# Half of an input projection made during the first scan, through device memory

## The chip, the core and the metric

The kernel runs on one core of a Trainium2 chip. The time is device microseconds of one execution, from three runs of the kernel before: 3769.12 us in the median (3767.9 to 3770.96). The profile comes from one further execution with the hardware profiler on.

The core has five engines, each with its own in-order queue of instructions: TensorE (PE in the profile; its weight loads are PEld), VectorE (DVE), ScalarE (ACT), GpSimd (POOL) and SyncE (SP, which here only issues DMAs). Sixteen DMA engines carry what is issued from SP and ACT.

## The reference

The input x holds 32 sequences of 256 tokens of 256 channels. First comes a selective state-space block, then two layers of local attention with a gated feed-forward, and the input is added at the end:

```python
xr, gate = jnp.split(x @ W_in.T, 2, axis=-1)          # 512 channels each
xr = xr + t_emb[:, None, :]
xc = silu(causal_depthwise_conv(xr, 4 taps) + b_conv)
xn = layernorm(xc)
Bm, Cm, dt = jnp.split(xn @ W_xproj.T, 3, axis=-1)    # 16 states each
...
h = jnp.clip(h * ad[:, :, None] + bd[:, :, None] * xt[:, None, :], -10.0, 10.0)
yt = jnp.einsum('bd,bdh->bh', ct, h)                  # 256 steps in order
...
return (y + D * xn) * silu(gate) @ W_out.T
# then, twice: attention over windows of 128 tokens, feed-forward with gelu
```

The scan over time is sequential: 256 steps for each sequence. All arithmetic that matters here is 32-bit.

## The kernel before

**Tiling.** The 32 sequences go in four groups of eight (`GB`). A scan step works on [128, 512]: 16 states times 8 sequences on the partitions, 512 channels along the free dimension. A group's 256 steps are cut into eight chunks (`NCH`) of 32 steps (`CH`). For each chunk, some 40 steps ahead of its first, the kernel loads x (`load_x`), projects it (`project`, four times for the convolution's half and four times for the gate's half), convolves, normalises, writes the normalised rows to device memory (`norm_out`, tensor `xnd`), and works out the factors of each step.

**A step.** `step` (line 660) is one custom VectorE instruction: it adds a scaled row to the state and clips it. The row of step t is the normalised token of eight sequences, repeated for 16 states. Normally `load_rows` (line 629) fetches it from `xnd` with a DMA of 256 KB that repeats it, and `scale_row` (line 650) scales it on ScalarE. During the first group's scan (`alone`), `by_tensor` picks steps with `t % NQ < XR`, that is two of every four, for another way: `spread_rows` (line 637) repeats the row with TensorE, two 32-row matmuls for two steps, out of a compact copy `xq` (`load_skip`), and ScalarE scales it out of PSUM. Row tiles (`xrep`) rotate through six buffers. `read_out` (line 672) turns the states of four steps into outputs, four matmuls of 32 columns each.

**Stages.** The scan of group 1 runs with nothing beside it. After it, attention and feed-forward of group g run beside the scan of group g+1. The last group's attention and feed-forward run alone.

**Order.** Each piece of the scan is put at a slot (`at(slot, function, ...)`), where slot s of a group stands beside step s; group g is shifted by 256 g slots (`scan_slots`). The second agenda of a group, lines 832 to 855, holds what a step needs of TensorE and of the row loads. `scan_to` advances the slots along the stages of attention and feed-forward. From this written order a planner fixes the order in each engine's queue and draws all waits; it may bring an instruction forward that has its inputs and its buffer (loads of the weights, put at slots from 100 on, stand at 10 to 32 us of the trace). It holds instructions back to each other's order where `keep_in_program_order` says so. A buffer of a tag with `bufs=n` is handed on when its last reader is done.

**Buffers that the change touches.** Tag `xg` (two buffers: the x of a chunk, which is read by the convolution's projections at slots s0 - 40 to s0 - 34 and by the gate's at s0 + 13 to s0 + 18), tag `rot` (four: `xq` in the first scan, rotary products later), tag `pT` (six: the weights of `spread_rows` in the first scan, attention's probabilities later), and the eight PSUM banks (`bank`).

Of the kernel before, what the change touches and what calls it, by code (L numbers as in the profile page):

```python
# [10 lines left out]
FP = mybir.dt.float32  # L11
# [8 lines left out]
P = 128  # L20
S = 256
DM = 256
KM = DM // P
DI = 512
NC_ = DI // P
NS = 16
GB = 8
CH = 32
NCH = S // CH
TB = P // GB  # L30
NQ = 4
# [3 lines left out]
XR = 2  # L35
TAPS = 4
# [16 lines left out]
def bc(ap, axis, n):  # L53

    ap = ap.unsqueeze(axis)
    shape = list(ap.shape)
    shape[axis] = n
    return ap.broadcast_to(shape)
# [15 lines left out]
def kernel(  # L74
# [29 lines left out]
    nc = tc.nc  # L104
    B = xT.shape[2]
    L = wqkv.shape[1]
    NG = B // GB

    const = ctx.enter_context(tc.tile_pool(name="const", bufs=1))
    def loaded(src, shape, name, q=None):  # L110
        t = const.tile(shape, FP, tag=name, name=name)
        (q or nc.scalar).dma_start(out=t, in_=src)
        return t
# [22 lines left out]
    w_in_sb = loaded(w_inT, [P, KM, 2 * DI], "w_in_sb", nc.sync)  # L136
# [26 lines left out]
    for j in range(NJ):  # L163
# [18 lines left out]
        out=mask_t[:, 0:W], in_=mask_t[:, 0:W], compare_op=ALU.is_ge, fill=MASKED_LOW,  # L182
# [3 lines left out]
        out=mask_t[:, W : 2 * W], in_=mask_t[:, W : 2 * W], compare_op=ALU.is_ge,  # L186
# [27 lines left out]
    for i in range(2):  # L214
        t = const.tile([P, NI * (P + GB)], FP, tag=f"ly{i}", name=f"ly{i}")
# [3 lines left out]
    def program(ctx, exact):  # L219
        rpool = ctx.enter_context(tc.tile_pool(name="res", bufs=1, reuse_waits="tile"))  # L220
        wpool = ctx.enter_context(tc.tile_pool(name="weights", bufs=1, reuse_waits="tile"))
        sp = ctx.enter_context(tc.tile_pool(name="sp", bufs=1, reuse_waits="tile"))
        sm = ctx.enter_context(tc.tile_pool(name="sm", bufs=2, reuse_waits="tile"))
        hp = ctx.enter_context(tc.tile_pool(name="hp", bufs=8, reuse_waits="tile"))
        xp = ctx.enter_context(tc.tile_pool(name="xp", bufs=6, reuse_waits="tile"))
        dp = ctx.enter_context(tc.tile_pool(name="dp", bufs=3, space=DRAM))
        ap_ = ctx.enter_context(tc.tile_pool(name="at", bufs=2, reuse_waits="tile"))
        aw = ctx.enter_context(tc.tile_pool(name="aw", bufs=3, reuse_waits="tile"))
        ps_w = ctx.enter_context(tc.tile_pool(name="psw", bufs=8, space=PSUM, reuse_waits="tile"))

        def bank(pool, tag, name):
            return pool.tile([P, DI], FP, tag=tag, name=name)
# [140 lines left out]
        def group_scan(g):  # L373
# [8 lines left out]
            alone = g == 0  # L382

            agendas = [{}]
            state = {"p": one}
            ck = [{} for _ in range(NCH)]

            def at(s, what, *args):
                agendas[-1].setdefault(s, []).append(partial(what, *args))
# [12 lines left out]
                ck[c]["ps", ch] = ps  # L402


            def load_x(c):
                xg = sp.tile([P, KM, GB, CH], FP, tag="xg", name="xg", bufs=2)
                for k in range(KM):
                    nc.sync.dma_start(
                        out=xg[:, k], in_=xT[:, k, b0 : b0 + GB, c * CH : (c + 1) * CH]
                    )  # L410
                ck[c]["xg"] = xg
                ck[c]["carry"] = sm.tile(
                    [P, NC_, GB, TAPS - 1], FP, tag="carry", name="carry"
                )

            def conv_in(c, ch):
                if ch == 0:
                    ck[c]["xc"] = sp.tile([P, NC_, GB * CH], FP, tag="xc", name="xc")
                ps = ck[c].pop(("ps", ch))
                xr = sp.tile([P, GB, TAPS - 1 + CH], FP, tag="xr", name="xr", bufs=2)  # L420
                if c == 0:
                    nc.gpsimd.memset(xr[:, :, 0 : TAPS - 1], 0.0)
                else:
                    nc.gpsimd.tensor_copy(xr[:, :, 0 : TAPS - 1], ck[c - 1]["carry"][:, ch])
                nc.vector.tensor_add(
                    xr[:, :, TAPS - 1 :],
                    ps.rearrange("p (b t) -> p b t", b=GB),
                    bc(cond_sb[:, ch, b0 : b0 + GB], 2, CH),
                )
                acc = sp.tile([P, GB, CH], FP, tag="acc", name="acc", bufs=2)  # L430
                nc.gpsimd.tensor_scalar(  # L431
                    acc, xr[:, :, 0:CH], wc_sb[:, ch, 0:1], bconv_sb[:, ch : ch + 1],
                    ALU.mult, ALU.add,
                )
                if c < NCH - 1:
                    nc.gpsimd.tensor_copy(ck[c]["carry"][:, ch], xr[:, :, CH:])
                ck[c]["xr", ch] = xr, acc
# [183 lines left out]
                return ck[c]["xnd"].rearrange("(b t) d -> b t d", b=GB)  # L621

            def by_tensor(t):
                return alone and t % NQ < XR

            def load_rows(c, t):
                xr = xp.tile([P, DI], FP, tag="xrep", name="xrep")
# [18 lines left out]
            def scale_row(c, t):  # L646
                if by_tensor(t):
                    ck[c]["rep", t] = xp.tile([P, DI], FP, tag="xrep", name="xrep")
                bx = ck[c]["rep", t]
                scaled = nc.scalar.activation(  # L650
                    bx, ck[c].pop(("bx", t), bx), AF.Copy, scale=ck[c]["beta"][:, t : t + 1]
                )
                if not alone:

                    tc.keep_in_program_order(scaled)
# [140 lines left out]
            for c in range(NCH):  # L796
                s0 = c * CH
                for hb in range(CH // TB):
                    s = s0 + hb * TB
# [5 lines left out]
                for ch in range(NC_):  # L805
                    at(s0 - 38 + 2 * ch, conv_in, c, ch)
                    at(s0 - 37 + 2 * ch, conv_taps, c, ch)
                    at(s0 - 36 + 2 * ch, conv_th, c, ch)
                    at(s0 - 35 + 2 * ch, conv_out, c, ch)
# [5 lines left out]
                for j in range(NJ):  # L815
                    s = s0 - 26 + 4 * j
# [15 lines left out]
            agendas.append({})  # L832
            for c in range(NCH):
                s0 = c * CH
                at(s0 - 43, load_x, c)
                for ch in range(NC_):
                    at(s0 - 40 + 2 * ch, project, c, ch)
                for ch, s in enumerate((13, 16, 17, 18)):
                    at(s0 + s, project, c, NC_ + ch)
                at(s0 - 27, raw_sums, c)  # L840
                for j in range(NJ):
                    at(s0 - 26 + 4 * j, norm_turn, c, j)
                at(s0 - 8, figures_out, c)
                for t in range(CH):
                    if not by_tensor(t):
                        at(s0 + t - 6, load_rows, c, t)
                    if by_tensor(t) and t % XR == 0:
                        at(s0 + t - 4, spread_rows, c, t)
                    at(s0 + t - 2, scale_row, c, t)
                for hb in range(CH // TB):  # L850
                    s = s0 + hb * TB
                    at(s - 9 if alone else s + 7, load_skip, c, hb)
                    at(s + 23, out_turn, c)
                for d in range(KM):
                    at(s0 + 43 + 2 * d, project_y, c, d)

            return agendas

        def scan_slots(groups):


            slots, scans = {}, [group_scan(g) for g in groups]
            for part in range(2):
                for i, agendas in enumerate(scans):
                    for s, what in agendas[part].items():
                        slots.setdefault(i * S + s, []).extend(what)
            for s in range(min(slots), max(slots) + 1):
                for what in slots.get(s, ()):
                    what()
                yield s  # L870


        ys, res, wt = {}, {}, {}

        def load_res(g, b):
            t = rpool.tile([P, KM, 1 + S], FP, tag=f"res{b}", name=f"res{b}")
# [90 lines left out]
        if exact:  # L967
# [4 lines left out]
                out=mask[:, 0:W], in_=mask[:, 0:W], compare_op=ALU.is_ge, fill=MASKED,  # L972
# [3 lines left out]
                out=mask[:, W : 2 * W], in_=mask[:, W : 2 * W], compare_op=ALU.is_ge, fill=MASKED,  # L976
# [425 lines left out]
        s0 = done[0]  # L1402
        group, reload = ST * L * GB, ST * (L * GB - GB + 6) + 2
        for t in range(max(stages) + 1):
# [3 lines left out]
            g, r = divmod(t + 1 + group - reload, group)  # L1408
# [10 lines left out]
    with tc.If(fits > 0) as which:  # L1419
        with ExitStack() as es:  # L1420
            program(es, False)
    with which.Else():
        with ExitStack() as es:
            program(es, True)
# [108 lines left out]
```

## Time and profile before

| | |
|---|---|
| median of three runs | 3769.12 us (3767.9 to 3770.96) |
| profiled execution, its own time | 3770.68 us |
| its span, first to last instruction | 3768.9 us |
| TensorE busy in the span | 3644.0 us (97%), granted clock 0.986 |
| VectorE busy | 2639.5 us (70%) |
| ScalarE busy | 2163.9 us (57%) |
| GpSimd busy | 1796.0 us (48%) |
| DMA, mean over the span | 103 GB/s, 387.53 MB |
| row loads (`xrep<-xnd`) | 896 of 256 KB |
| step 1 of the first scan starts at | 54.3 us |

A row of the profile names line, engine and operation, then output and inputs by tile name, the shape and the count; after the bar come busy time, the mean in ns, and the time that the engine was idle just before such instructions, with what ended the idle time. Busy time of TensorE counts the modelled end of each matmul, and where matmuls overlap, their common time once. A 32-bit matmul leaves two records.

### The profile page before, as it was taken

The page shows a single profiled execution, that of the slowest core. Times are in us where ns is not written, and L with a number is a line of the kernel's source. Part 1 is how long each engine was busy: PE and PEld are TensorE (multiplying, and loading weights), DVE is VectorE, ACT ScalarE, POOL GpSimd, SP SyncE. Part 2 cuts the span into 40 slices and gives each one's busy share as a digit, 9 for nine tenths or more (in the row PEclk, how much of TensorE's full clock was granted, in tenths as well). Part 3 has the DMA queues.
Part 4 walks back from the last instruction along what each step waited for, and adds up shares of the span by engine and source line. Part 5 has one row for each costly group of instructions (what it writes and reads, how often), then busy time and mean ns, then how long its engine had stood idle before and what let it go on. Part 6 is the DMA issues. An engine that isn't in the chain of part 4 may idle for free.

```text
span 3768.9 us, 57035 instructions
## 1 busy us (share of the span) xinstructions
PE 3644.0 (97%) x20028; PEld 2255.5 (60%) x20028; DVE 2639.5 (70%) x5177; ACT 2163.9 (57%) x3769; POOL 1796.0 (48%) x1776
## 2 busy tenths in 40 slices
PE   7999989999999999999999999999999999999998
PEld 3333345666666666666666666666666666666666
DVE  6988888788778777777777777777776444444443
ACT  3555556666666666656666665666566444444442
POOL 4443365544455455545445555545454444433441
PEclk8999999999999999999999999999999999999999
DMA  5444555344454545444444545444353111011101
GB/s 149 114 119 117 135 155 135 101 119 116 116 130 123 145 120 150 106 108 114 112 120 110 147 119 138 115 101 116 108 130 109 54 43 50 12 29 38 29 26 35
DMA packets 396250, 387.53 MB, mean 103 GB/s; under 512 B 176355, under 2 KB 256052, under 8 KB 395828
## 3 DMA queue, kind: packets, MB, share of 16 engines
q1 hardware_dynamic: 311506, 371.80, 37.1%
q10 hardware_dynamic: 84450, 12.01, 2.0%
q8 instruction: 161, 2.64, 0.3%
q14 instruction: 133, 1.09, 0.1%
HBM read 348.05 MB, written 34.08 MB: 101 GB/s over the span
## 4 chain that ended last, share of the span: by engine, by line
PE 68%; DVE 16%; POOL 6%; ACT 4%; issue 3%; DMA 3%; SPq 0%; ACTq 0%; POOLq 0%; DVEq 0%
PE ps_qkv L907 14%; PE pa L1246 13%; PE po_f L1274 8%; PE y L672 5%; DVE h L660 5%; PE ps_wo L957 4%; PE sc L1113 4%; PE ov L1151 3%; DVE acc L442 3%; PE ps_out L750 3%; PE ps_in L395 3%; PE tr_qk L946 2%; POOL rn L939 2%; PE rs L1132 2%; PE sc L1106 2%
## 5 line engine op out<-in xcount | busy, mean ns | idle before, releaser
L660 DVE CUSTOM_DVE_ANT_0 h<-h,xrep,lim 128x512 f32<-128x512 f32 x1024 | 936.5, 915 | 238.7 <-ACT xrep L650 207.7
L907 PE MATMUL ps_qkv<-qkv,res 128*128 128x512 f32 x1536 | 712.1, 600 | 23.6 <-DVE ag L1262 18.2
L650 ACT ACTIVATE xrep<-xrep,beta 128x512 f32<-128x512 f32 x896 | 622.5, 717 | 113.2 <-DMA xrep<-xnd 71.0
L1246 PE MATMUL pa<-hT,w 128*128 128x256 f32 (+1 forms) x3072 | 684.4, 385 | 0.3 <-DVE zT L741 0.2
L1246 PEld LDWEIGHTS pa<-hT,w 128*128 128x128 f32 (+1 forms) x3072 | 498.4, 178 | 159.6 <-issue 44.1
L931 POOL TENSOR_TENSOR rot<-rot,swp 128x512 f32<-128x512 f32 x256 | 335.2, 1309 | 368.9 <-DVE swp L928 223.7
L939 POOL TENSOR_TENSOR rn<-ss,neg_half 128x8 f32<-128x8 f32 x256 | 460.3, 1798 | 17.8 <-DVE ss L937 7.9
L907 PEld LDWEIGHTS ps_qkv<-qkv,res 128*128 128x128 f32 x1536 | 278.0, 191 | 300.5 <-issue 260.5
L1274 PE MATMUL po_f<-ag,w 128*128 128x256 f32 (+1 forms) x1536 | 386.8, 393 | 13.5 <-DVE ag L1262 8.9
L1203 POOL TENSOR_TENSOR rstd<-ve,neg_half 128x1 f32<-128x1 f32 x128 | 81.2, 634 | 645.7 <-DVE ve L1201 642.8
L672 PE MATMUL y<-h,ly 128*32 128x512 f32 x2048 | 372.7, 620 | 10.6 <-DVE h L660 9.8
L1274 PEld LDWEIGHTS po_f<-ag,w 128*128 128x128 f32 (+1 forms) x1536 | 273.0, 189 | 120.0 <-issue 54.6
L1262 DVE SCALAR_TENSOR_TENSOR ag<-pa,b_sb,ag 128x256 f32<-128x256 f32 (+1 forms) x448 | 212.5, 474 | 171.6 <-ACT ag L1254 168.0
L940 POOL TENSOR_TENSOR rot<-rot,rn 128x512 f32<-128x512 f32 x256 | 301.1, 1176 | 20.0
L1254 ACT ACTIVATE ag<-pa,b_sb 128x256 f32<-128x256 f32 x320 | 150.7, 471 | 268.1 <-PE pa L1246 266.0
L395 PE MATMUL ps_in<-xg,w_in_sb 128*128 128x256 f32 x1024 | 282.8, 407 | 19.1 <-DMA xg<-in_xT_dram 14.9
L920 ACT ACTIVATE sq<-ps_qkv 128x512 f32<-128x512 f32 x256 | 151.7, 596 | 236.5 <-PE ps_qkv L907 200.1
L395 PEld LDWEIGHTS ps_in<-xg,w_in_sb 128*128 128x128 f32 x1024 | 189.9, 198 | 142.4 <-issue 41.2
L442 DVE SCALAR_TENSOR_TENSOR acc<-xr,wc_sb,acc 128x256 f32<-128x256 f32 x384 | 189.5, 496 | 91.7 <-POOL acc L431 89.6
L923 DVE TENSOR_TENSOR rot<-ps_qkv,rc_sb 128x512 f32<-128x512 f32 x256 | 175.3, 685 | 82.9 <-ACT sq L920 82.9
L957 PE MATMUL ps_wo<-oT,wo 128*128 128x256 f32 x1024 | 231.6, 379 | 0.0
L450 ACT ACTIVATE th<-acc 128x256 f32<-128x256 f32 x128 | 53.0, 414 | 308.3 <-DVE acc L442 255.0
(146 smaller groups left out, 5672.4 us busy)
## 6 DMA issues: line engine op xcount, KB each, us to landing
xrep<-xnd SPq DMA_DIRECT2D x896, 256.0 KB
rb<-inv SPq DMA_DIRECT2D x128, 256.0 KB
xnd<-xn SPq DMA_DIRECT2D x64, 256.0 KB
qkv<-in_wqkv_dram SPq DMA_DIRECT2D x24, 512.0 KB
xd<-xnd SPq DMA_DIRECT2D x192, 64.0 KB
w<-in_w_dram SPq DMA_DIRECT2D x80, 128.0 KB
xg<-in_xT_dram SPq DMA_DIRECT2D x64, 128.0 KB
ys<-yo ACTq DMA_DIRECT2D x64, 128.0 KB
```

The costliest lines, as they stand in the source:

```text
L395: nc.tensor.matmul(ps, w_in_sb[:, k, ch * P : (ch + 1) * P], ck[c]["xg"][:, k], start=(k == 0), stop=(k == KM - 1),)
L442: nc.vector.scalar_tensor_tensor(acc, xr[:, :, k : k + CH], wc_sb[:, ch, k : k + 1], acc, ALU.mult, ALU.add,)
L650: scaled = nc.scalar.activation(bx, ck[c].pop(("bx", t), bx), AF.Copy, scale=ck[c]["beta"][:, t : t + 1])
L660: nc.vector._custom_dve(TENSOR_ADD_SAT, out=h_new, in0=state["h"], in1=bx, s0=ck[c]["lim"][:, 0, t : t + 1], s1=ck[c]["lim"][:, 1, t : t + 1],
L672: nc.tensor.matmul(ck[c]["y", hb][32 * q : 32 * q + 32, :], ly[hb % 2][:, 32 * t : 32 * t + 32], ck[c].pop(("h", hb * TB + t)), start=(i = ...
L907: nc.tensor.matmul(ps, res[b][:, k, t0 : t0 + W], wt["qkv", a][:, k], start=(k == 0), stop=(k == KM - 1),)
L931: nc.gpsimd.tensor_add(rot, rot, swp)
L939: nc.gpsimd.tensor_tensor(rn, ss, neg_half, ALU.pow)
L940: nc.gpsimd.tensor_mul(rot, rot, bc(rn, 2, DH))
L957: nc.tensor.matmul(po[:, d], wt["wo", 0][:, c, d * P : (d + 1) * P], oT[:, c, :], start=(c == 0), stop=(c == NC_ - 1),)
L1246: nc.tensor.matmul(pg if x else pa, wt["w1", m][:, k, x], self.h[:, k], start=(k == 0), stop=(k == KM - 1),)
L1274: nc.tensor.matmul(self.po[:, d], wt["w2", 0][r0 : r0 + n, m, d * P : (d + 1) * P], self.ag[m][r0 : r0 + n], start=(m == 0), stop=(m == le ...
```

## The change

Three things are done.

1. For groups 2 to 4 (the code's g = 1 to 3) the convolution's half of the input projection is no longer made ahead of each chunk. 48 units of work are put evenly over the first scan's slots -30 to 220: `ahead_load` fetches the x of a chunk (for every second unit, two DMAs of 128 KB), `ahead_project` makes two of the four channel blocks of a chunk into one PSUM bank, `ahead_copy` copies the bank to SBUF on ScalarE, and `ahead_put` stores it to device memory, 256 KB a unit. Later, at slots s0 - 44 and s0 - 42 of the chunk, `load_projected` fetches both units of the chunk into buffers of tag `xg`, and `conv_in` reads its addend there and not from PSUM.
2. `load_x` of these groups moves from slot s0 - 43 to s0 + 6, since only the gate's half still needs x; the small tile `carry` is made in `conv_in`.
3. `by_tensor` takes `t % (2 * NQ) < XR`: in the first scan two of every eight rows are spread by TensorE, and six of eight are loaded.

```diff
+            def ahead_load(u):
+                if u % 2 == 0:
+                    gg, c = 1 + u // 2 // NCH, u // 2 % NCH
+                    t = ap_.tile([P, KM, GB, CH], FP, tag="rot", name="xa", bufs=4)
+                    for k in range(KM):
+                        nc.sync.dma_start(
+                            out=t[:, k],
+                            in_=xT[:, k, gg * GB : (gg + 1) * GB, c * CH : (c + 1) * CH],
+                        )
+                    state["xa", u // 2] = t
+            def ahead_project(u):
+                ps = bank(ps_w, "w", "ps_a").rearrange("p (r n) -> p r n", r=2)
+                for r in range(2):
+                    ch = 2 * (u % 2) + r
+                    for k in range(KM):
+                        nc.tensor.matmul(
+                            ps[:, r],
+                            w_in_sb[:, k, ch * P : (ch + 1) * P],
+                            state["xa", u // 2][:, k],
+                            start=(k == 0),
+                            stop=(k == KM - 1),
+                        )
+                state["pa", u] = ps
+            def ahead_copy(u):
+                t = aw.tile([P, 2, GB * CH], FP, tag="pT", name="xs_a", bufs=6)
+                nc.scalar.copy(t, state.pop(("pa", u)))
+                state["ta", u] = t
+            def ahead_put(u):
+                d = dp.tile([P, 2, GB * CH], FP, tag=f"ahead{u}", name=f"ahead{u}", bufs=1)
+                nc.sync.dma_start(out=d, in_=state.pop(("ta", u)))
+                projected[u] = d
+            def load_projected(c, i):
+                t = sp.tile([P, 2, GB * CH], FP, tag="xg", name="xp", bufs=2)
+                nc.sync.dma_start(out=t, in_=projected[((g - 1) * NCH + c) * 2 + i])
+                for r in range(2):
+                    ck[c]["ps", 2 * i + r] = t[:, r]
...
             def by_tensor(t):
-                return alone and t % NQ < XR
+                return alone and t % (2 * NQ) < XR
...
-                at(s0 - 43, load_x, c)
-                for ch in range(NC_):
-                    at(s0 - 40 + 2 * ch, project, c, ch)
+                at(s0 - 43 if alone else s0 + 6, load_x, c)
+                if alone:
+                    for ch in range(NC_):
+                        at(s0 - 40 + 2 * ch, project, c, ch)
+                else:
+                    for i in range(2):
+                        at(s0 - 44 + 2 * i, load_projected, c, i)
...
+            if alone:
+                n = (NG - 1) * NCH * 2
+                for u in range(n):
+                    s = -30 + u * (NCH * CH) // n
+                    at(s - 5, ahead_load, u)
+                    at(s, ahead_project, u)
+                    at(s + 2, ahead_copy, u)
+                    at(s + 4, ahead_put, u)
```

More of the change, by code (lines that the diff above doesn't have):

```diff
@@ L411, in load_x @@
                 ck[c]["xg"] = xg
-                ck[c]["carry"] = sm.tile(
-                    [P, NC_, GB, TAPS - 1], FP, tag="carry", name="carry"
-                )
             def conv_in(c, ch):
                 if ch == 0:
+                    ck[c]["carry"] = sm.tile(
+                        [P, NC_, GB, TAPS - 1], FP, tag="carry", name="carry"
+                    )
                     ck[c]["xc"] = sp.tile([P, NC_, GB * CH], FP, tag="xc", name="xc")
@@ L870, in scan_slots @@
                 yield s
-        ys, res, wt = {}, {}, {}
+        ys, res, wt, projected = {}, {}, {}, {}
         def load_res(g, b):
```

## The prediction

> **What bounds the kernel now.** I read three things in this order: the table of engine times by stage, to see where TensorE has room; the sequence of TensorE instructions in two of the stages, for the price of what moves; and the groups and waits of the first scan, for what sets its pace. The stages are: set-up (0 to 54 us), the first scan with nothing beside it (54 to 440), the hand-over (to 620), the scans of groups 2 to 4 beside attention and feed-forward (to 2930), and the last group's attention. Each row gives length, busy us of each engine, clock, DMA share and GB/s.
>
> ```profile
> core 0: us, PE busy (x) PEld busy (x) DVE busy (x) ACT busy (x) POOL busy (x), PEclk, DMA share, GB/s
> 0.00:54.00 54.00, 29.18 (x116) 22.02 (x116) 24.24 (x71) 8.04 (x17) 21.49 (x64) 0.75 0.67 174
> 54.00:440.00 386.00, 355.46 (x1315) 134.14 (x1315) 345.30 (x623) 227.99 (x425) 157.77 (x194) 0.94 0.45 118
> 440.00:620.00 180.00, 159.11 (x726) 77.08 (x726) 154.24 (x290) 99.02 (x182) 106.07 (x110) 0.92 0.55 145
> 620.00:2930.00 2310.00, 2271.88 (x13151) 1462.10 (x13150) 1752.70 (x3413) 1447.79 (x2525) 1177.05 (x1131) 1.00 0.46 120
> ```
>
> In the long stage TensorE is busy 98% and VectorE 76%: TensorE's work is the time. In the first scan TensorE is at 92% and VectorE at 89%: neither is free. The change moves TensorE work from the first kind of stage into the second, so everything turns on how much of it the first scan swallows.
>
> Prices, from the TensorE sequence of the main stage and of the first scan (start, length with its tail, instruction, records; every f32 matmul is two records):
>
> ```profile
> 2027.85 1.99 PE L395 MATMUL ps_in<-xg,w_in_sb 128*128 128x256 f32 x8
> 2029.68 0.38 PE L1223 MATMUL tp_hn<-ident,hn 128*128 128x128 f32 x2
> ...
> 301.98 1.13 PE L637 MATMUL bx<-xq,rep_w 32*128 32x512 f32 x4
> 303.04 1.05 PE L672 MATMUL y<-h,ly 128*32 128x512 f32 x4
> 304.02 1.12 PE L637 MATMUL bx<-xq,rep_w 32*128 32x512 f32 x2
> 305.07 1.05 PE L672 MATMUL y<-h,ly 128*32 128x512 f32 x2
> ```
>
> Eight projection records take 1.83 us from start to next start. Two spread rows (x4) take 1.06 us, but one (x2) takes 1.05 as well. The same holds for read-out (y): two matmuls cost no more than one when they stand together.
>
> Groups of the first scan (count, busy us, mean ns, idle before):
>
> ```profile
> L660 DVE CUSTOM_DVE_ANT_0 h<-h,xrep,lim 128x512 f32<-128x512 f32 x250 | 231.7, 927 | 8.2 <-DVE h L660 1.9 <-PE ps_in L395 0.6 <-PE y L672 0.3
> L672 PE MATMUL y<-h,ly 128*32 128x512 f32 x488 | 144.4, 648 | 4.8 <-DVE h L660 4.0
> L650 ACT ACTIVATE xrep<-xrep,beta 128x512 f32<-128x512 f32 x127 | 88.9, 715 | 73.6 <-DMA xrep<-xnd 60.1 <-DVE beta L598 4.4 <-DVE h L660 3.9
> L637 PE MATMUL bx<-xq,rep_w 32*128 32x512 f32 x252 | 80.8, 639 | 0.0
> ```
>
> and what the queue of SyncE (which issues every row load) waits for there (us, times, longest):
>
> ```profile
> SPq L629 <- DVE h L660: 147.8, 77, 7.0
> SPq L535 <- POOL xn L531: 49.3, 16, 3.3
> ...
> SPq L689 <- DMA xnd<-xn: 10.6, 6, 2.3
> ```
>
> So row loads mostly wait for one of the six row buffers, which is harmless; the waits for the normalised rows, twice a chunk, hold up every load behind them, and ScalarE then waits for rows (60.1 us in all). The chain of waits gives 9.5% of the first scan, 37 us, to row loads, and some 40% to TensorE.
>
> **What the Trainium skill says.** "Perfetto Trace Analysis", Identifying the Most-Contended Engine: matmul busy time says little on how near TensorE is to its limit, the share of weight loads says more. Here that is 63% in the main stage and 35% in the first scan, so the first scan has more room than its 92% suggests. "TensorE: Matmul & The Clock Gate", Part 3, Packing small matmuls: matmuls on different row groups run at once, and one of 32 rows takes as long as one of 128; the 1.06 and 1.05 us above agree. "DMA: Bandwidth & Descriptors", Anatomy of one DMA: DMA engines wait on no semaphore, the issuing sequencer does; the waits above show it. The same page, Specifications, puts the limit from device memory near 358 GB/s per core; the trace's 118 GB/s at a share of 0.45 extrapolates to 262.
>
> **The change, part by part.**
>
> *Removed from the main stage.* The convolution's half for groups 2 to 4 is 3 x 8 chunks x 4 x 2 matmuls = 384 records. Some 336 of them (21 of the 24 chunks; the stage has 672 records of this line, half of them for the gate) lie after 620 us; the other three chunks are made around the end of the first scan and cancel in part. 336/8 x 1.83 = 77 us of TensorE; by shares of busy time (0.263 us a record there) it would be 88. VectorE, next, is at 76%, so nearly all of it should show; I take 95% for the waits that stay: **-73 us**. Ends: -88, and -38 if half is lost to order.
>
> *Added in the first scan.* 48 units of eight records at 1.83 to 2.0 us, say 1.87: 90 us. Their start slots run from -30, so five or six fall into set-up, where TensorE is half idle (10 us); some 8 us of the last two chunks' own projections go away. Net 72 us inside the first scan.
>
> *Spread by TensorE halved.* 64 fewer rows, 32 pairs x 1.06 = -34 us of TensorE (busy shares would say -40). In their place 64 row loads.
>
> *TensorE in the first scan*: 355 + 72 - 34 = 393 us in a window of 386. At the 98% of the main stage that needs 401: +15. It can be less: read-out takes 144 us because much of it goes out as single matmuls right after a step; a fuller queue lets them stand together. It can be +38, if the 92% are already the limit.
>
> *ScalarE*: 48 copies of 128x512 out of PSUM; the nearest row is the scaled row out of PSUM at 0.68 us: 33 us on 228 of 386. Hidden under ScalarE's 41% idle time, but it stands before row scalings: up to 0.7 us of delay at a time. I take +2; uncovered it would be 33.
>
> *Queue of SyncE*: 64 row loads, 48 loads of x and 48 stores, at 0.52 us an issue (row loads' median): 83 us more on 111 (213 issues). It fits in 386, since most of its waiting is for buffers. But each store waits for ScalarE's copy, two slots earlier, with row loads queued behind it.
>
> *DMA*: 16.8 MB of rows, 12.6 MB of stores, 6.3 MB of x: 92 GB/s more, so about 210 GB/s or a share of 0.8. Loads take longer (2 KB packets take 84 ns median, 162 at the 75th percentile already). With three of four rows by DMA, a hold-up of the queue is bridged by fewer TensorE rows. Price from both sides: 0 if six buffers cover it, and +67 if exposed time per row doubles with rows 1.5 times as many (33 to 37 us becomes about 100). I take +8.
>
> *Set-up*: six units and their loads before step 0: +2 (0 to 10).
>
> *Main stage, added*: 48 loads of 256 KB in 2400 us (5 GB/s), awaited six slots later; VectorE's addition (0.415 us out of PSUM) reads SBUF instead. Nothing. In the ring of two x buffers the second load of group 2's first chunk waits until its first is used, two slots before need: at most 3 us, once. I take 0.
>
> Sum: -73 + 15 + 2 + 8 + 2 = **-46 us**. The profiled execution took 3770.68 us (span 3768.9); against it 3725, against the median of 3769.12 about **3723**.
>
> **Rivals.**
>
> A, the forecast: the main stage gives 73, the first scan takes back 27. 3723, its own range 3700 to 3750.
>
> B, the first scan swallows it all: its TensorE is 92% busy by stretched waits, weight loads 35%. Then -73 + 4 gives 3700. Against it: TensorE's queue in the first scan shows hardly a gap.
>
> C, TensorE becomes the first scan's sole bound with the stretch it has now: -73 + 38 + 12 gives 3746.
>
> D, the slow side: rows arrive late. Place: SyncE's queue in the first scan, behind the stores of normalised rows and the new stores; price +67, with TensorE's +15, +10 for set-up and +2: -73 + 94 gives 3790. It decides once each of eight chunks grows by more than 9 us, six steps; the loads are already 37 us of the chain. Against it: most of SyncE's waits are for buffers, not for data.
>
> E, the gain isn't there: the main stage's order is bound by chains through VectorE and ScalarE, so half the removed time comes back (-38 + 27): 3758. Against it: 98% busy.
>
> **Chances.** A 0.45, B 0.15, C 0.12, D 0.20, E 0.08. A measurement of this kernel tells some 0.2% (7.5 us) from no change: faster means under 3761.6. A, B, C and half of E give 0.76, less 0.06 for their tails: 0.70. Same 0.07: half of E and 0.03 of the tails. Slower 0.23: D and the other 0.03. For 8 in 10 I leave out the half of B below 3694 and the upper half of D: 3694 to 3788.
>
> **What would show it.** In the after-profile: the first scan's length (386 now) between 395 and 425; TensorE's records of the projection line halved after 620 us and that stage shorter by 65 to 80; TensorE above 95% busy in the first scan; ScalarE's waits for row loads there (60.1) under 100. Wrong if ScalarE's or VectorE's waits on row loads exceed 130 us, if a chunk of 32 steps takes over 57 us (48 now), or if the main stage keeps its length.

## The result, and the profile after

The changed kernel takes 3756.36 us in the median of nine runs (3750.83 to 3763.89), the kernel before 3770.96 (3767.9 to 3773.69) in runs beside it. The ratio is 0.9963, 95% interval 0.9954 to 0.9972: 14.6 us or 0.4% faster, where 46 us had been forecast. The profiled execution took 3750.83 us (span 3748.7); it is the fastest of the nine, so differences of spans come out some 6 us larger than differences of medians.

The stages of the changed kernel, with the same windows and columns as the first table of the prediction:

```profile
core 0: us, PE busy (x) PEld busy (x) DVE busy (x) ACT busy (x) POOL busy (x), PEclk, DMA share, GB/s
0.00:54.00 54.00, 32.54 (x148) 24.73 (x148) 24.89 (x73) 10.07 (x21) 22.19 (x66) 0.91 0.78 205
54.00:440.00 386.00, 357.06 (x1498) 178.71 (x1496) 331.92 (x608) 246.82 (x451) 157.46 (x193) 0.96 0.73 201
440.00:620.00 180.00, 153.27 (x688) 67.83 (x687) 160.04 (x297) 104.37 (x195) 106.63 (x106) 0.96 0.60 163
620.00:2930.00 2310.00, 2250.34 (x12949) 1422.87 (x12949) 1799.79 (x3443) 1463.55 (x2546) 1223.59 (x1143) 0.99 0.46 125
```

The first scan holds 183 records of TensorE more than before and TensorE is hardly busier (357 against 355 us); DMA has gone from 118 to 201 GB/s. In the long stage TensorE has fallen from 2272 to 2250 us of 2310.

Fixed windows show no lengths, so I mark the stages by the starts of the scan's own step instructions (steps 0, 256 and 1023; between 256 and 1023 lie groups 2 to 4):

| us | before | changed | forecast | measured |
|---|---|---|---|---|
| up to step 0 | 54.3 | 57.3 | +2 | +3.0 |
| steps 0 to 256 | 397.9 | 405.0 | +15 +8 +2 = +25 | +7.1 |
| steps 256 to 1023 | 2476.1 | 2445.5 | -73 | -30.6 |
| after step 1023 | 840.6 | 840.8 | 0 | +0.2 |
| span | 3768.9 | 3748.7 | -46 | -20.2 |

So the first scan cost less than forecast, and the gain is missing in the long stage. Within it, group 2 gained 16 us (756.1 to 740.1), group 3 only 5 (866.3 to 861.6) and group 4 10 (853.8 to 843.7).

The groups of the first scan after the change (count, busy us, mean ns, idle before; steps 0 to 256):

```profile
L693 ACT ACTIVATE xrep<-xrep,beta 128x512 f32<-128x512 f32 x193 | 137.9, 719 | 97.4 <-DMA xrep<-xnd 90.3 <-DVE xr L468 3.0 <-issue 2.8
L715 PE MATMUL y<-h,ly 128*32 128x512 f32 x512 | 132.9, 636 | 7.2 <-DVE h L703 6.1 <-DVE ve L551 0.6
L422 PE MATMUL ps_a<-xa,w_in_sb 128*128 128x256 f32 x344 | 86.8, 392 | 0.7 <-DMA xa<-in_xT_dram 0.6
L680 PE MATMUL bx<-xq,rep_w 32*128 32x512 f32 x124 | 40.0, 655 | 0.0
L433 ACT COPY xs_a<-ps_a 128x512 f32<-128x512 f32 x43 | 24.8, 577 | 13.5 <-PE ps_a L422 12.3 <-PE y L715 0.7 <-issue 0.6
```

The work made ahead (L422) takes 86.8 us, halved spreading (L680) 40.0 in place of 80.8, and read-out (L715), with the same 512 records, 132.9 in place of 151.0. ScalarE waits 90.3 us for rows, where it waited 61.2 before over the same steps.

Now the long stage: what waits on rows in group 3 (us in total, times, longest). Before:

```profile
DVE h L660 <- ACT xrep L650: 88.5, 63, 2.9
```

After:

```profile
DVE h L703 <- ACT xrep L693: 99.2, 55, 3.5
ACT xrep L693 <- DMA xrep<-xnd: 52.3, 23, 3.7
ACT xrep L693 <- DVE beta L641: 22.3, 8, 3.0
```

The second and third lines are new: before, ScalarE's scalings wait in this group neither for row loads nor for the factors of a chunk (`beta`). The second is not a slow DMA; the chain that ended last shows where it comes from. One place of it in group 3 (start, length, what), around the change from one chunk to the next:

```profile
1518.00 0.82 DVE h L703
1518.82 0.03 issue
1518.84 0.81 DVE h L703
1519.65 0.03 DVE ag L1317
1519.68 3.55 DMA xrep<-xnd
...
1523.31 0.72 ACT xrep L693
1524.04 0.47 ACT oT L1213
1524.51 0.63 ACT xrep L693
1525.14 0.03 issue
1525.16 0.82 DVE h L703
```

The step at 1518.84 is number 30 of its chunk, the one at 1525.16 is number 31. Between them lie a whole row load and two scalings. The load is not that of row 31: that was issued at 1507.34, five loads earlier. It is the load of the row five places later, row 4 of the next chunk. In ScalarE's queue the scaling of row 4 stands ahead of the scaling of row 31 (numbers are those of the built instructions; `beta_13323` belongs to the old chunk, `beta_14367` to the next; lines between them are left out):

```
1751  xrep_14314 <- xrep_14314, beta_13323    row 29
1752  xrep_14452 <- xrep_14452, beta_14367    row 2 of the next chunk
1755  xrep_14526 <- xrep_14526, beta_14367    row 4 of the next chunk
1756  oT_14481   <- ov_14492                  attention
1757  xrep_14370 <- xrep_14370, beta_13323    row 31
```

There are six row buffers. Row 4's load takes over the buffer of row 30, so it can only be issued when step 30 is done. Then its 3.55 us, its scaling, attention's copy and row 31's scaling follow one another while row 31 lies ready in SBUF. The Trainium skill, "Perfetto Trace Analysis", section Tensor Engine Instruction (MATMUL, LD_WEIGHTS), says that ScalarE executes strictly first in, first out; the trace agrees, with a loaded row standing behind one that isn't, and ScalarE idle for 3.24 us ahead of row 4's scaling.

The third line has the same shape, three places apart. Row 0 of the next chunk is scaled ahead of row 29, and its scaling waits for that chunk's factors. In the place shown ScalarE is idle for 2.74 us until they are there, scales row 0 from 1515.66, copies twice for attention and scales row 29 from 1517.34; step 29 follows at 1518.00. This happens once in each of the eight chunks of group 3.

Counting in the built queues, for groups 2 to 4, how many row scalings stand behind a scaling of a later row, and by how many places the latest is ahead:

```
                1    2    3    4    5 places     all
before         78   40   49    1    0            168
changed        67   57   70   18   31            243
```

28 of the 31 that are five places late are in groups 3 and 4, the groups that gained least: 14 times row 25, behind row 30, and 14 times row 31, behind row 4 of the next chunk.

### The profile page after: what moved, and what is told of

It reads as the page before. It is cut to its first block, busy times and chain, and to the rows that moved or that the text cites. A ratio compares the mean times of both kernels' runs of the same rounds, so it can differ in the third digit from the quotient of the medians.

```text
span 3748.7 us, 57254 instructions
## 1 busy us (share of the span) xinstructions
PE 3601.1 (96%) x19900; PEld 2242.4 (60%) x19900; DVE 2669.6 (71%) x5177; ACT 2195.4 (59%) x3817; POOL 1834.9 (49%) x1776
## 4 chain that ended last, share of the span: by engine, by line
PE 62%; DVE 16%; POOL 7%; ACT 6%; DMA 5%; issue 3%; SPq 0%; ACTq 0%; DVEq 0%; POOLq 0%
PE ps_qkv L962 12%; PE pa L1301 12%; PE po_f L1329 7%; DVE h L703 6%; PE y L715 4%; PE ps_wo L1012 4%; DMA xrep<-xnd 4%; PE sc L1168 4%; PE ov L1206 3%; PE ps_out L793 2%; ACT xrep L693 2%; DVE acc L485 2%; PE tr_qk L1001 2%; PE ps_in L395 2%; POOL acc L474 2%
## 5 line engine op out<-in xcount | busy, mean ns | idle before, releaser
L703 DVE CUSTOM_DVE_ANT_0 h<-h,xrep,lim 128x512 f32<-128x512 f32 x1024 | 948.2, 926 | 269.2 <-ACT xrep L693 238.8
L693 ACT ACTIVATE xrep<-xrep,beta 128x512 f32<-128x512 f32 x960 | 674.1, 719 | 333.0 <-DMA xrep<-xnd 235.9
L962 PE MATMUL ps_qkv<-qkv,res 128*128 128x512 f32 x1536 | 727.1, 610 | 45.2 <-DVE ag L1317 30.1
L1301 PEld LDWEIGHTS pa<-hT,w 128*128 128x128 f32 (+1 forms) x3072 | 492.9, 178 | 183.7 <-issue 66.5
L715 PE MATMUL y<-h,ly 128*32 128x512 f32 x2048 | 354.9, 612 | 12.9 <-DVE h L703 11.7
L1177 ACT ACTIVATE pT<-sc 128x512 f32<-128x512 f32 x384 | 208.5, 596 | 32.2 <-PE sc L1168 30.7
L1168 PE MATMUL sc<-qT,kT 64*128 64x128 f32 (+1 forms) x2048 | 221.5, 345 | 0.0
L1012 PEld LDWEIGHTS ps_wo<-oT,wo 128*128 128x128 f32 x1024 | 194.5, 190 | 27.2 <-PE y L715 0.8
```

What stands on the lines that cost most here:

```text
L693: scaled = nc.scalar.activation(bx, ck[c].pop(("bx", t), bx), AF.Copy, scale=ck[c]["beta"][:, t : t + 1])
L703: nc.vector._custom_dve(TENSOR_ADD_SAT, out=h_new, in0=state["h"], in1=bx, s0=ck[c]["lim"][:, 0, t : t + 1], s1=ck[c]["lim"][:, 1, t : t + 1],
L715: nc.tensor.matmul(ck[c]["y", hb][32 * q : 32 * q + 32, :], ly[hb % 2][:, 32 * t : 32 * t + 32], ck[c].pop(("h", hb * TB + t)), start=(i = ...
L962: nc.tensor.matmul(ps, res[b][:, k, t0 : t0 + W], wt["qkv", a][:, k], start=(k == 0), stop=(k == KM - 1),)
L1012: nc.tensor.matmul(po[:, d], wt["wo", 0][:, c, d * P : (d + 1) * P], oT[:, c, :], start=(c == 0), stop=(c == NC_ - 1),)
L1168: nc.tensor.matmul(banks[r][:, i, :], kT[rows, i0 + i, kw * W : (kw + 1) * W], qT[rows, i0 + i, kw * W :], start=False, stop=(i == n - 1),)
```

## The experiments

Each ran beside the kernel before on the same chip; ratios are to it, with 95% intervals. "Row order" below always means an issue order in ScalarE's queue, with no wait added. Lengths of a stage are from each run's profiled execution, and they differ even where the order of the scalings is the same: the long stage of run 2 is 4.5 us longer than that of before (2480.6 and 2476.1), and that of run 3, whose profiled execution is the slowest of its ten, 14 us longer than that of the changed kernel (2459.6 and 2445.5).

**1. The removal alone.** The kernel before, without the convolution's half of the projection in groups 2 to 4.

```diff
             def project(c, ch):
+                if ch < NC_ and not alone:
+                    ck[c]["ps", ch] = ck[c]["xg"][:, ch % KM].rearrange("p b t -> p (b t)")
+                    return
```

> The kernel before, with the convolution's half of the projection of groups 2 to 4 left out: the convolution reads the x tile in its place, so the values of groups 2 to 4 are not the reference's. Nothing is added to the first scan and no load is added to the main stage. Theory 1 (TensorE's work is the time of the main stage, and the gain was lost to the new loads and stores): steps 256 to 1023 get shorter by about 73 us, the time falls to about 3697. Theory 2 (the main stage is held by the order of the other engines' queues as soon as TensorE is relieved): they get shorter by only about 30 us, as in the changed kernel, and the time is about 3740.

Measured: 3775.49 us (3772.56 to 3784.66), ratio 1.0006 (0.9997 to 1.0015). TensorE has 77 us less to do, and nothing at all is gained; the long stage is 2480.8 us. The time lies above what either theory expected. That speaks against the added loads as the place where the gain went, and run 4, which has them in it, settles it. The queue of this kernel has the late rows too: 28 of them five places late in groups 3 and 4, as in the changed kernel. The planner thus orders them so in both kernels in which this TensorE work is gone. (Run 6 shows that this kernel also carries a cost of its own.)

**2. The quarter of rows alone**, in the kernel before.

```diff
             def by_tensor(t):
-                return alone and t % NQ < XR
+                return alone and t % (2 * NQ) < XR
```

> The third part of the change alone: in the first scan a quarter of the rows, not a half, is spread by TensorE; nothing is projected ahead. If TensorE holds back the first scan (34 us of its work go away): shorter by 5 to 15 us. If row loads hold it back: longer by 5 to 15 us. The main stage stays the same under both.

Measured: 3771.2 us (3766.64 to 3781.86), ratio 0.9993 (0.9986 to 1.0001); steps 0 to 256 take 394.2 us, 3.7 less than before; neither expectation, 5 to 15 us either way, holds. Steps 0 to 256 as in the first table:

```profile
55.70:449.90 394.20, 346.84 (x1222) 127.85 (x1220) 355.50 (x652) 237.22 (x432) 175.93 (x204) 0.97 0.60 161
```

TensorE's busy time falls by 20 us (366.5 before) and not by 34, because read-out now takes 184.7 us in place of 151.0, and ScalarE's waits for row loads rise from 61.2 to 98.8. The stage hardly moves: before the change TensorE is not the first scan's only limit. The order of the scalings in groups 2 to 4 is that of before.

**3. The work made ahead, without the quarter**: the changed kernel with the spreading of before.

```diff
-                return alone and t % (2 * NQ) < XR
+                return alone and t % NQ < XR
```

> The first two parts of the change, without the third: projected ahead, half of the rows spread by TensorE. If TensorE is the bound of the first scan, it gets longer than the changed kernel's 405 us by 20 to 34 us (about 3780 in all). If the first scan has room on TensorE, by under 10 us (about 3762). The main stage as in the changed kernel.

Measured: 3781.97 us (3776.51 to 3788.94), ratio 1.0022 (1.0012 to 1.0031). Steps 0 to 256, length and busy times as in the first table:

```profile
60.60:486.60 426.00, 385.29 (x1668) 188.48 (x1666) 355.32 (x649) 253.54 (x472) 165.93 (x202) 0.97 0.58 151
```

28 us longer than before and 21 longer than the changed kernel, as expected if TensorE is the bound; the quarter of rows pays for three quarters of what the work made ahead costs, and without it the change would be a loss of 8 us. That TensorE alone makes the difference is not shown, though. It is busy for 90% of the stage; ScalarE's waits for row loads rise here too, from 61.2 us before to 88.8, with no more rows loaded; and 97 scalings of the first scan are late in this queue, up to three places, against 45 before and 34 in the changed kernel, up to two.

**4. Row scalings in order, in the changed kernel.** Each scaling of groups 2 to 4 is queued behind the scaling before it, in addition to the pin that stands there.

```diff
                     tc.keep_in_program_order(scaled)
+                    if "scaled" in state:
+                        tc.add_manual_dep(
+                            scaled.ins,
+                            state["scaled"],
+                            mybir.DependencyInfo(
+                                mybir.DependencyClass.NoSync, mybir.DependencyReason.DATA
+                            ),
+                            reason="rows in order",
+                        )
+                    state["scaled"] = scaled.ins.name
```

> The changed kernel, with the row scalings of groups 2 to 4 held in the order of the steps in ScalarE's queue. In the changed kernel, rows 25 to 31 of a chunk stand up to five places behind later rows, some of them of the next chunk. Theory 2a (this order is where the main stage's gain was lost): about 1.5 to 2 us less for each of 24 chunks, 36 to 48 us, the time falls to about 3715. Theory 2b (the bound is elsewhere, in the chain of the convolution on VectorE and GpSimd): within 10 us of the changed kernel.

Measured: 3695.03 us (3691.39 to 3698.58), ratio 0.9793 (0.9777 to 0.981): 61 us less than the changed kernel, and the fastest kernel of this study together with two near relatives of it (8 and 9). Theory 2b falls; 2a is right about the place and put the price too low (36 to 48 us). Steps 256 to 1023, and group 3 of them:

```profile
466.40:2850.20 2383.80, 2342.99 (x13475) 1467.51 (x13476) 1925.17 (x3672) 1547.25 (x2697) 1317.80 (x1230) 0.99 0.50 131
1203.60:2029.90 826.30, 819.67 (x4783) 523.00 (x4782) 666.35 (x1285) 540.93 (x941) 467.74 (x435) 1.00 0.50 131
```

In group 3 TensorE is busy 99.2%; in the changed kernel it is 832.21 of 861.60 us, 96.6%, and before 851.41 of 866.20, 98.3%. The wait for row loads is gone from that group, that for `beta` is down to 2.7 us, once, and this is what is left of the steps' waits for scalings:

```profile
DVE h L713 <- ACT xrep L693: 56.6, 39, 2.4
```

A rival is that the planner, asked for one more order, drew the other queues anew as well. Laid beside the changed kernel's, the built queue of TensorE is the same, instruction for instruction. In ScalarE's 191 instructions of 3683 stand elsewhere, in VectorE's 72 of 5165, in SyncE's 6 and in GpSimd's 3; in run 8, which is as fast, it is 88, 20, 4 and 3.

**5. The same order in the kernel before.**

> The kernel before, with one thing added: the row scalings of groups 2 to 4 are held in the order of their steps in ScalarE's queue (issue order only, no wait). Theory O (the order of the row scalings costs time only where TensorE has been relieved; in the kernel before TensorE is busy 98% of the main stage and is the limit by itself): little, 10 to 25 us faster than before, 3745 to 3760. Rival P (the disorder costs the same in both kernels, and the projection made ahead has no part in it): as much as in the changed kernel, 55 to 65 us faster, 3705 to 3715; then the changed kernel's gain with rows in order is again only some 15 us.

Measured: 3761.31 us (3754.77 to 3763.92), ratio 0.9964 (0.9949 to 0.9979): 11 us faster. Theory O holds and P falls: the disorder of before costs some 10 us (steps 256 to 1023: 2465.7 in place of 2476.1), the disorder of the changed kernel six times as much. With rows in order in both, the change takes the long stage from 2465.7 to 2383.8 us, by 82.

**6. The removal alone, with rows in order.**

> The kernel before without the convolution's half of the projection in groups 2 to 4 (x itself stands in its place, so the values differ), as in the run without that half, and with the row scalings of groups 2 to 4 in the order of their steps. Nothing is made ahead. Theory O: with the order held, the removed work of 77 us shows nearly in full against the run before_rows_in_order: 60 to 80 us shorter, at 3680 to 3690. Rival P: no_conv_projection was no faster than before, so this is no faster than before_rows_in_order, within 10 us. A third reading, Q (the path through VectorE, ScalarE and TensorE of attention binds next): 30 to 50 us shorter.

Measured: 3709.65 us (3704.67 to 3713.97), ratio 0.9828 (0.9811 to 0.9845): 52 us less than run 5. P falls, O's 60 to 80 us are not reached, and the number is that of Q, but the reason given under Q isn't supported, since run 4 is 33 us shorter in the long stage (2383.8 against 2416.8) with the same TensorE work in it. The same gap lies between runs without rows in order: 2480.8 in run 1 and 2445.5 in the changed kernel. So this control carries some 34 us of its own. In it GpSimd waits 48.2 us (21 times) in group 3 to copy the convolution's first columns until VectorE has done with the buffer, in run 4 20.7 us (15 times). One step of each chunk is longer in both such runs, that from 21 to 22: 5.6 us in run 1 and 5.8 here, 2.1 in the changed kernel and 1.9 in run 4. That these waits are the 34 us was not tested.

**7 and 8. Which late rows cost.** The order of run 4 for some rows of each chunk only.

```diff
-                    if "scaled" in state:
+                    if "scaled" in state and not 2 <= t < 26:
```

Run 8 has `not 6 <= t < 26` in this place.

> The changed kernel, where in groups 2 to 4 only the scalings of the rows 26 to 31, 0 and 1 of each chunk are held behind the scaling before them; rows 2 to 25 stay free. The rows 25 to 31 are those that the changed kernel scales late and the kernel before does not. Theory N (the new late rows at a chunk's end are what swallowed the gain): at least half of the 61 us that the full order gives, 3710 to 3730. Rival M (late rows anywhere in the chunk cost alike; this order leaves 202 of 277 late rows): a quarter, 3735 to 3745. Under neither over 3765.

Run 7 measured: 3730.02 us (3723.83 to 3735.25), ratio 0.9881 (0.9863 to 0.9898). That is 26 of the 61 us, between the two expectations and right under neither. Its queue explains it: row 31 stayed five places late (14 rows in groups 3 and 4), now behind rows 2 to 4 that were left free. Row 29 no longer stands behind row 0, and the waits for `beta` in group 3 are down to 2.7 us, once.

> The changed kernel, where in groups 2 to 4 the scalings of the rows 26 to 31 and 0 to 5 of each chunk are held behind the scaling before them. What is left out of order in these groups are rows at most three places late (101 of them; the changed kernel has 243, some of them five places late). Theory R (the cost is that of rows five places late, because with six row buffers the load of the row that stands ahead can only start when the step before the late row is done, so that its 3.6 us lie bare; rows up to three places late cost next to nothing): 3690 to 3706, with the step from row 30 to 31 at 2.8 us and not 6.5. Rival U (each late row costs alike, 61 us by 239 rows, 0.26 us): the 97 more than in the full order cost 25 us, 3716 to 3724.

Run 8 measured: 3695.25 us (3692.07 to 3701.81), ratio 0.9792 (0.9776 to 0.9808). It keeps 101 late rows, none more than three places, and is as fast as the full order. U falls: late rows as such cost nothing to speak of. R holds for what this run leaves late, but not as a rule about places, since row 29 is three places late in the changed kernel and does cost. Runs 7 and 8 divide the 61 us: 26 come back with the rows 26 to 1 in order, row 29 among them, and 35 more when row 31 is no longer five places late.

The time from one step to the next, in us, at the steps where the kernels differ (median over twelve chunks, the second to seventh of group 3 and the first to sixth of group 4; the last column is the whole chunk of 32, from step 0 to the next chunk's):

| from step | 26 | 28 | 30 | 0 | 6 | 22 | chunk |
|---|---|---|---|---|---|---|---|
| before | 6.64 | 5.56 | 4.85 | 5.70 | 1.29 | 3.57 | 108.6 |
| before, rows in order (5) | 6.64 | 5.56 | 4.24 | 5.50 | 1.29 | 3.58 | 107.7 |
| changed | 2.36 | 5.06 | 6.54 | 3.31 | 2.90 | 7.38 | 107.9 |
| rows 26 to 1 in order (7) | 2.36 | 3.55 | 6.63 | 3.31 | 1.64 | 7.38 | 105.3 |
| rows 26 to 5 in order (8) | 2.36 | 3.55 | 2.79 | 3.93 | 2.71 | 7.38 | 103.1 |
| all rows in order (4) | 2.36 | 3.55 | 2.79 | 3.93 | 2.71 | 7.38 | 103.1 |

Against the full order, the step from 30 to 31 loses 3.75 us in the changed kernel, one bare row load (3.55 us in the chain above); that from 28 to 29 loses another 1.5, the wait for the next chunk's factors. (Even in runs 4, 7 and 8 one row 29 is left behind a row 0, at the end of group 3, and its step takes 5.06 us there too.) Other steps give a little back. Over the eight chunks of group 3, 4.8 us each make 38; measured are 35 (861.6 to 826.3). Row 25 is five places late as well, but the step before its own takes 9.8 us in all kernels from the changed one down, whether row 25 is late or not: its load is covered.

**9. Rows in order in the first scan too.** The same lines outside the condition that leaves the first scan out.

> The changed kernel with the row scalings in the order of their steps in the first scan too, where 34 of 256 are late in its queue. If the first scan is bound by TensorE (as the run with twice the rows spread says), its length stays within 4 us of 408.5 and the time within 5 us of 3695. If late rows cost there as they do later, at some 0.2 us for each, the first scan is 7 us shorter and the time 3686 to 3690.

Measured: 3695.47 us (3694.81 to 3703.11), ratio 0.9801 (0.9784 to 0.9819); steps 0 to 256 take 407.4 us against 408.5 in run 4. The first scan of the changed kernel is not bound by the order of its scalings, whose late rows are at most two places late.

**10 to 12. Where the disorder comes from.** The code pins each scaling of groups 2 to 4 behind the ScalarE instruction written just before it, often one of attention; two neighbouring rows can so hang on two instructions that the planner places far apart. Without the pins, the planner puts all scalings of these groups in order by itself, in both kernels.

```diff
-                    tc.keep_in_program_order(scaled)
```

Run 10, the changed kernel without the pins:

> The changed kernel without the line that pins each row scaling of groups 2 to 4 behind the ScalarE instruction written before it; nothing in its place. The planner then puts all of these scalings in the order of their steps by itself. Theory S (the pins make the late rows, and the late rows swallowed the gain): as the run with rows in order, 3685 to 3705. Rival T (the pins are needed, because unpinned scalings are put ahead of attention's own ScalarE work and TensorE waits for that): more than 15 us over that run, 3710 to 3760.

Measured: 3926.68 us (3916.67 to 3936.28), ratio 1.0413 (1.0389 to 1.0438).

Run 11, the changed kernel with the chain of run 4 in place of the pins:

> The changed kernel with each row scaling of groups 2 to 4 held behind the row scaling before it, in place of the pin behind the ScalarE instruction written before it. Theory S: within 8 us of the kernel without the pins, since the order of the rows is the same. Rival T: as in the kernel without the pins, 3710 to 3760; if only this one is at 3695, the chain does something other than keep the order.

Measured: 3929.42 us (3922.72 to 3941.71), ratio 1.0434 (1.0416 to 1.0453).

Run 12, the kernel before without the pins:

> The kernel before without the pins of the row scalings in groups 2 to 4. Theory S: as before_rows_in_order, 3755 to 3765, since TensorE is full there and the order matters little. Rival T: slower than before, 3775 to 3800.

Measured: 3981.16 us (3978.47 to 3982.94), ratio 1.0558 (1.0541 to 1.0576).

Theory S falls: the order of the rows alone does not help, whether the planner finds it (runs 10 and 12) or it is stated (run 11). T holds in direction and had put the price far too low. Waits in group 3 of the changed kernel without pins:

```profile
ACT xrep L693 <- DMA xrep<-xnd: 169.5, 75, 7.8
DVE ag L1317 <- ACT ag L1309: 139.3, 39, 5.7
```

In the changed kernel with its pins these are 52.3 and 10.9 us. Unpinned, scalings stand in the queue ahead of attention's and the feed-forward's ScalarE work before their rows are there, and that work waits behind them; TensorE is busy for 92% of the group. The pins prevent this (they are worth 170 us in the changed kernel, 212 before and 234 with rows in order) and make rows late as a side effect. The two orders are needed together, pin and chain, as in run 4.

## Why the prediction was wrong, step by step

The direction was right, the size was not: 3723 forecast, 3756 measured. It lies in the range only because the range reached out to the slower cases, so that is no support for the reasoning.

**Removed from the main stage: the step that failed.** "VectorE, next, is at 76%, so nearly all of it should show; I take 95%." The TensorE price was right: 77 to 88 us, and with rows in order in both kernels TensorE's busy time in the long stage falls by 74 us and the stage shortens by 82 (runs 4 and 5). What failed is that the rest would keep its place. The planner works out every queue anew. With 77 us less on TensorE it put row 31 of the chunks in groups 3 and 4 five places back in ScalarE's queue, where six buffers let the loop of step, load, scaling and step close on itself, and row 29 behind the first row of the next chunk, whose factors were not there yet. The disorder cost 61 us, against 10 before; 82 + 10 - 61 gives the 31 that were measured. The prediction read busy shares and what SyncE waits for, and not the order of the scalings beside the number of row buffers.

**Rival E** named the right place, the main stage's order, and hit the size (3758), with a chance of 0.08. Its mechanism was broader than the true one: not chains through VectorE and ScalarE in general, but two rows in 32. "Against it: 98% busy" was the error in weighing it. That share said that TensorE had no room, not that the time would follow when room was made: in group 3 it fell from 98.3% to 96.6%, while the two late rows held the time.

**Added in the first scan, and the spread rows halved.** Forecast +15 for TensorE, +38 at worst, 0 if read-out stands together more. Measured +7.1 for the whole stage, with +8 for rows and +2 for ScalarE in the forecast besides. TensorE's busy time rose by 6.7 us (366.5 to 373.2), where 38 had been forecast. Read-out, which the sum left at 144, is the largest term that was off, 18 of the 31 us: it took 151.0 us over steps 0 to 256 before, 132.9 in the changed kernel and 114.7 in run 3. So the fuller queue did let matmuls stand together, the possibility named with the +15: single read-out matmuls, with other work on both sides, number 48 before, 28 in the changed kernel, 14 in run 3 and 60 in run 2. Made ahead with the spreading of before, the stage is +28 (run 3); halving the spreading gives 21 of these back (run 3 against the changed kernel) and 3.7 alone (run 2). Rival C's price falls, but not because the stage lost its stretch: TensorE is busy for 92% of it in both kernels, and 6.7 us more at 92% are about the +7.1. (At that stretch C's 38 us would have been 41.) The price of +8 for rows cannot be told apart from this.

**ScalarE and DMA in the first scan.** Copies took 577 ns, priced 680. DMA ran at 201 GB/s and a share of 0.73, expected 210 and 0.8. "Loads take longer" is not borne out packet by packet: those of 2 KB in the first scan took 84 ns in the median and 98 at the 75th percentile before (162, as the prediction has it, is near the 90th, 165), and 84 and 94 after. ScalarE waits 90.3 us for rows over steps 0 to 256 (61.2 before), under the 100 that were set as the mark. Rival D falls: this is the queue that it named, in the first scan of the changed kernel (us, times, longest):

```profile
SPq L578 <- POOL xn L574: 25.3, 8, 4.7
SPq L411 <- POOL xd L745: 11.7, 6, 3.2
SPq L438 <- ACT xs_a L433: 7.6, 12, 1.1
```

The stores of normalised rows (L578) hold the queue for half of what they did (49.3), the new stores (L438) for 7.6 us in all. Of the marks set, the first scan's chunk (50.6 us, 57 as the limit) and ScalarE's wait held; "TensorE above 95%" failed, with 373.2 of 405.0 us, 92%, as before, and so did "shorter by 65 to 80" for the main stage.

**Set-up**: +2 forecast, +3.0 measured.

**Main stage, added.** "At most 3 us, once" for the second load of a chunk's products was wrong as an account of SyncE's queue: `load_projected` waits there twice in every chunk, in the eight of group 3 for 66.5 us (10.5 at the longest) and 34.2 us (4.6). But run 4 has the same waits (66.1 and 33.7 us) beside TensorE at 99.2%, so nothing points to them as a cost; a kernel without them wasn't run. VectorE's addition took 0.417 us out of SBUF in group 3, 0.413 out of PSUM before: nothing, as said.

**What stays open.** Why the planner, relieved of TensorE work, picks just this order was not traced. What bounds the first scan was not separated into TensorE, row loads and ScalarE's order. Nor was it shown what makes up the 34 us of the two runs without the projection, or whether more row buffers would cure the late row as well.

## What to carry to other kernels

Where a planner fixes the order of the queues, removing work changes the order of what stays; read the queues of the new build before trusting a difference of busy times. With n buffers in a ring, an item that stands d places late in a first-in-first-out queue waits for a load that can only start n - d steps before it: at five places of six buffers the load's whole latency lay bare at the step from 30 to 31, while the rows up to three places late in run 8 cost nothing. But a late item also waits for whatever else the item ahead of it waits for, as row 29 did for the next chunk's factors. When TensorE's share falls after TensorE's work was cut and the time does not, compare the steps of a period one by one with those of a build whose queue is in order. Beside the kernel before alone, the step from 22 to 23 grew most here (3.57 to 7.38 us), and it stays as long in the fastest kernel.

## What the runs showed beyond that

In run 3, 344 matmul records of 85.3 us were added to the first scan, some 14 us of its own projections went, and its busy TensorE time rose by only 19 us (366.5 to 385.3). The largest part of the difference is read-out, whose 512 records took 36 us less as fewer of its matmuls stood alone. In run 2, with less work beside it, the same read-out took 34 us more. So the busy time of such matmuls is not a fixed price; it depends on what is queued beside them. And an order that costs nothing to state, one scaling behind another, was worth more here (61 us) than the whole change without it (15 us).
